# Attention with heads of width 96: the product with Wo as seven products of block sums, and a later load of the expert layer's last weights

## Chip, cores and metric

The kernel runs on one core of a Trainium2 chip. The metric is the time of one execution on the device in microseconds; runs are summed up by their median. The profile is one execution recorded by the hardware profiler, so its time is its own and is compared with itself.

## What is computed

The program is a chain of eight residual layers over 1024 tokens (16 sequences of 64) of width 512, each on a layer-normalised input. Two of them matter here, the expert layer (`L2_ffn`) and the attention after it (`L3_xattn`); the last layer (`L3_ffn`, weights of 3 bits) follows.

```python
# L2_ffn: 64 experts of rank 16, the best 16 of a token gated by a softmax
h = jnp.einsum('nd,krd->nkr', xf, A)
out = jnp.einsum('nkr,kdr->nd', h * G[:, :, None], B)      # times SCALING = 2

# L3_xattn: 16 query heads, 4 key/value heads of width 96
hidden = jnp.concatenate([context, latents], axis=1)       # 64 + 64 rows
q = (latents @ Wq.T).reshape(b, q_len, 16, 96)
k, v = (hidden @ Wk.T), (hidden @ Wv.T)                    # 4 heads each
attn = softmax(q k / sqrt(96));  out = attn v              # (b, q_len, 1536)
return out @ Wo.T                                          # 1536 -> 512
```

With four query heads to a key/value head, one key/value head gives 4 x 96 = 384 rows of Wo, three chunks of 128.

## The kernel before

**Tiles and lanes.** The tokens are eight tiles of 128 (two sequences each). The residual stream `k.x[t]` stays in SBUF. Two generators are traced into one program: lane b (`side`) does the first layers for all tiles and then the later ones for tiles 0 to 3; lane a (`main`) does the wide attention (`normed_attention`, L752) for all tiles and then the later layers for tiles 4 to 7. `merged` (L1737) interleaves them: each `yield` gives a cost in us, and the other lane is advanced until it has used as much. TensorE executes in exactly this order; the other engines and the queues are ordered by a scheduler, so a DMA goes out when its room is free and its queue (SP's) reaches it, which can be well ahead of its place in the code. Lane b is some 150 us ahead, so at the end lane a runs alone.

**Rooms.** Each lane has four PSUM banks in a ring and, for weights, four pages of 2048 floats a partition (`Lane.page`, L120); a page is free once every instruction that was given its last contents is done. Other tiles come from pools opened by each layer; `bufs` says how many there are of a tag.

**Seven products.** The expert layer's two products are already formed in Strassen's manner: over a pair of tiles and the two halves of the width, eight block products become seven. `block_sums` (L1234) forms, on GpSimd, four sums of the blocks of each weight part, and writes them to DRAM; this runs once, in lane b, one operation for each step of its `small_head_attention` (58 steps; eight parts take 33). `LoraWeights.load` (L1297) fetches a part as two DMAs, 384 KB of blocks and 512 KB of sums. `stream_sums` (L1358) and `hidden_sums` (L1420) form the sums of the activations, `Seven.products` (L1272) the products in the order a11, a12, s2, s3, s1, a22, s4, two to a bank, and `output` (L1438) adds them to the two tiles on VectorE, with one copy by ScalarE.

**The expert layer** (`lora_experts`, L1307) has parts 0 to 3 for its first product and 4 to 7 for its second. It loads 0 to 5 at its start (4 and 5 into tiles of their own) and 6 and 7 after `hidden(1, 0)`, which ends the use of parts 0 and 1. The first half of `output(0)` comes right after `hidden(1, 1)`, then `turn(1, 0)` and `turn(1, 1)` (transpositions of the gated hidden values), then the rest.

**The attention** (`packed_attention`, L1556) computes values for all tiles (with `l3a_wv`), then runs over units (head, pair of tiles), eight in a lane, head by head: `units = [(h, t) for h in range(NKV) for t in tiles[::2]]`. In iteration n it does `keys` of unit n, `turn_weights` of n-2, `scores` of n-1, `queries` of n, `project_both` of n-3 and `values` of n-2. Heads 0 to 2 carry a third of head 3's keys with them, so head 3 has no product of keys. `head_weights` loads a head's query and key weights and its rows of Wo (`l3a_o`, 768 KB) into two pages. `values` writes `aP`, three chunks for four sequences; `project` (through `Attention.project`, L742) multiplies one tile's three chunks with 128x512 of Wo into one bank, and VectorE adds the bank to `k.x[t]`. After the loop come the last unit's two `project`s, between them the pieces of the last layer (`Q3Linear`, L1498): `weights(c)` on VectorE, `norm`, `turn`, and `product` with the DMA out.

Of the kernel before, what the change touches and what calls it, by code (L numbers as in the profile page):

```python
# [8 lines left out]
F32 = mybir.dt.float32  # L9
# [9 lines left out]
P = 128  # L19
# [1270 lines left out]

class LoraWeights:

# [4 lines left out]
    def load(self, n, room=None):  # L1297
        if n in self.parts:
            return
        w = self.ln.page("w_l2f", 7 * W2) if room is None else room  # L1300
        half = 3 * W2
        self.ln.nc.sync.dma_start(w[:, :half], self.src[n, :, :half])
        self.ln.nc.sync.dma_start(w[:, half:], self.kept[n])
        self.parts[n] = w


def lora_experts(ln, tiles, weights, w_r):  # L1307
# [6 lines left out]
    with ExitStack() as es:  # L1314
        pool = ln.pool(es, "l2f")
        for n in range(4):
            weights.load(n)
        for n in range(4, 6):
            weights.load(n, pool.tile([P, 7 * W2], F32, tag=f"w{n}", name="w_l2f", bufs=1))
        wr = w_r.rearrange("p (c n) -> p c n", c=NC)  # L1320
# [37 lines left out]
        def stream_sums(p):  # L1358
            t, u = pairs[p]
            blocks = [k.kvT[:, c : c + 2, v, 1:3, :] for v in (t, u) for c in (0, 2)]  # L1360
            a11, a12, a21, a22 = blocks
            s = pool.tile([P, 4, 2, 2, S], F32, tag="s", name="sx", bufs=1)
            nc.gpsimd.tensor_tensor(s[:, 0], a21, a22, ALU.add)
            nc.gpsimd.tensor_tensor(s[:, 1], s[:, 0], a11, ALU.subtract)
            nc.gpsimd.tensor_tensor(s[:, 2], a11, a21, ALU.subtract)
            nc.gpsimd.tensor_tensor(s[:, 3], a12, s[:, 1], ALU.subtract)
            lhs[p] = {
                f"s{i + 1}": (lambda e, i=i: s[:, i, e].rearrange("p b s -> p (b s)"))
                for i in range(4)
            }  # L1370
            lhs[p]["a11"] = lambda e: k.stream(e, t)
            lhs[p]["a12"] = lambda e: k.stream(2 + e, t)
            lhs[p]["a22"] = lambda e: k.stream(2 + e, u)
# [64 lines left out]
        def output(p):  # L1438
            x = [k.x[v].rearrange("p (j n) -> p j n", j=2) for v in pairs[p]]

            def add(v, j, src):
                nc.vector.scalar_tensor_tensor(
                    x[v][:, j], src, SCALING, x[v][:, j], ALU.mult, ALU.add
                )

            m = Seven(ln, lhs.pop(p), [weights.parts[4 + e] for e in range(4)], "ps_o")
            s = pool.tile([P, 2, W2], F32, tag="u", name="uo")
            p1, p2 = m.products(2)
            nc.scalar.copy(s[:, 0], p1)
            add(0, 0, p1)  # L1450
            add(0, 0, p2)
            yield 3.45
            p6, p7 = m.products(2)
            nc.vector.tensor_tensor(s[:, 1], s[:, 0], p6, ALU.add)
            nc.vector.tensor_tensor(s[:, 0], s[:, 1], p7, ALU.add)
            yield 3.45
            p5, p4 = m.products(2)
            nc.vector.tensor_tensor(s[:, 1], s[:, 1], p5, ALU.add)
            add(1, 1, p5)
            add(1, 0, p4)  # L1460
            add(0, 1, s[:, 1])
            add(1, 1, s[:, 0])
            add(1, 0, s[:, 0])
            yield 3.45
            (p3,) = m.products(1)
            add(0, 1, p3)
            yield 1.7

# [12 lines left out]
        yield from turn(0, 0)  # L1481
        yield from hidden(1, 0)
        for n in range(6, 8):
            weights.load(n)
        yield from turn(0, 1)
        hidden_sums(0)
        yield from hidden(1, 1)
        out = output(0)
        yield next(out)
        yield next(out)  # L1490
        yield from turn(1, 0)
        yield from turn(1, 1)
        hidden_sums(1)
        yield from out
        yield from output(1)


class Q3Linear:  # L1498
# [5 lines left out]

    def load(self):
        nc, ln = self.ln.nc, self.ln
# [9 lines left out]
        self.r = r.rearrange("p (c j n) -> p c j n", c=NC, j=2)  # L1516
        self.bias = self.pool.tile([P, D], F16, tag="b16", name="b16", bufs=1)
        nc.sync.dma_start(self.bias, bias.partition_broadcast(P))
        self.wT = ln.page("wT_l3f", NC * D).rearrange("p (c n) -> p c n", c=NC)
        self.kept = {}  # L1520

    def weights(self, c):
        nc = self.ln.nc
        w, low, high = self.wT[:, c, :], self.r[:, c, 0, :], self.r[:, c, 1, :]
        nc.vector.tensor_tensor(w, high, low, ALU.subtract)
        nc.vector.scalar_tensor_tensor(
            w, self.q3[:, c * D : (c + 1) * D], 1.0 / 7.0, w, ALU.mult, ALU.mult
        )
        nc.vector.tensor_tensor(w, w, low, ALU.add)
# [14 lines left out]
    def product(self, t):  # L1544
# [3 lines left out]
        for c in range(NC):  # L1548
            nc.tensor.matmul(
                ps, lhsT=xT[:, c, :], rhs=self.wT[:, c, :], start=c == 0, stop=c == NC - 1  # L1550
            )
# [3 lines left out]

def packed_attention(ln, tiles, w_in, w_v, last):  # L1556

# [5 lines left out]
    with ExitStack() as es:  # L1563
# [31 lines left out]
        def head_weights(h):  # L1595
            if h < NKV and h not in heads:
                n_q, n_k = NC * G * HD, NC * P
                n = n_q + (n_k if h < NJ else 0)
                wa, wb = ln.page(f"l3a_w{h}", n), ln.page(f"l3a_o{h}", NJ * D)
                nc.sync.dma_start(wa, w_in[h, :, :n])  # L1600
                nc.sync.dma_start(wb, w_in[h, :, n_q + n_k :])
                heads[h] = (
                    wa[:, :n_q].rearrange("p (c n) -> p c n", c=NC),
                    wa[:, n_q:].rearrange("p (c n) -> p c n", c=NC) if h < NJ else None,
                    wb.rearrange("p (g n) -> p g n", g=NJ),
                )

        def keys(u):
            h, t = u
            if t == tiles[0]:  # L1610
                head_weights(h)
                head_weights(h + 1)
            four = k_last[:, 2 * (t - tiles[0]) : 2 * (t - tiles[0]) + 4, :]
# [49 lines left out]
        def values(u):  # L1663
            h, t = u
            d = kept[u]
            aP = pool.tile([P, NJ, 4, S], F32, tag="aP", name="aP")
            for i, pT in enumerate(d.pop("pT")):
# [9 lines left out]

        def project(u, i):
            h, t = u
            aP = kept[u]["aP"]  # L1680
            chunks = [
                aP[:, j, 2 * i : 2 * i + 2, :].rearrange("p b s -> p (b s)") for j in range(NJ)
            ]
            at.project(t + i, chunks, heads[h][2])

        def project_both(u):
            for i in range(2):
                project(u, i)

        linear = Q3Linear(ln, pool, *last)  # L1690
        units = [(h, t) for h in range(NKV) for t in tiles[::2]]
        for n in range(len(units) + 2):
            for lag, step, cost in [
# [3 lines left out]
                (0, queries, 5.2),  # L1697
                (3, project_both, 5.2),
                (2, values, 1.7),
            ]:  # L1700
                if n == len(units) + 1 and step == project_both:

# [3 lines left out]
                if 0 <= n - lag < len(units):  # L1706
                    own = step(units[n - lag])
                    yield cost if own is None else own
            if n == len(units):
                linear.load()  # L1710

# [4 lines left out]
        for c in range(2, 4):  # L1716
            linear.weights(c)
            yield 1.0
        project(units[-1], 0)
        yield 2.6  # L1720
        linear.norm(three)
        linear.turn(one)
        yield 0.5
        project(units[-1], 1)
        yield 2.6
        linear.norm(four)
        linear.turn(two)
        yield 0.5
        for t, ahead in zip(tiles, (three, four, None, None)):
            linear.product(t)  # L1730
# [48 lines left out]
def decoder_kernel(ctx: ExitStack, tc: tile.TileContext, i: dict, out: bass.AP):  # L1779
# [6 lines left out]
    kept_w = kept.tile([P, NC, D], BF16, tag="wT", name="wT_d")  # L1786
    kept_s = [kept.tile([P, 4 * W2], F32, tag=f"s{n}", name=f"sums_d{n}") for n in range(8)]

# [45 lines left out]
    def last_layers(ln, tiles, weights):  # L1834
        yield from lora_experts(ln, tiles, weights, routers[0])
        yield from packed_attention(
            ln, tiles, i["l3a_w"], i["l3a_v"], [i["l3f_q"], i["l3f_r"], i["l3f_b"], out]
        )

    def side():  # L1840
# [7 lines left out]
        with ExitStack() as es:  # L1848
            sums = block_sums(b, b.pool(es, "sums"), i["l2f_w"], kept_s)
            weights = LoraWeights(b, i["l2f_w"], kept_s)  # L1850
            for cost in small_head_attention(b, halves[0], i["l2a_w"], weights):
# [6 lines left out]
    def main():  # L1858
# [6 lines left out]
        yield from mxfp4_ffn(a, halves[1], None, i["l1f_b"], kept_w)  # L1865
        weights = LoraWeights(a, i["l2f_w"], kept_s)
        yield from small_head_attention(a, halves[1], i["l2a_w"], weights)
# [9 lines left out]
def laid_out(a):  # L1877
# [62 lines left out]
    parts = [blocks(w_a[:, D * j : D * (j + 1)], e) for j in range(2) for e in range(2)]  # L1940
    i["l2f_w"] = np.stack(parts + [blocks(w_b, e) for e in range(4)])
    w = [a[f"L3_xattn_W{n}"].T for n in "qkvo"]
    i["l3a_w"] = per_head(w[0], w[1], None, w[3], 96, 4)
    i["l3a_v"] = chunks(w[2])
# [24 lines left out]
```

## Time and profile before

| | |
|---|---|
| runs | 1619.85, 1620.28, 1628.03 us; median 1620.28 us |
| profiled execution | 1624.97 us, its span (first to last instruction) 1622.9 us |
| busy share of the span | TensorE 96%, VectorE 61%, ScalarE 38%, GpSimd 36% |
| granted TensorE clock, mean | 0.989 |
| lane b: block sums on GpSimd | 867 to 917 us |
| lane b: expert layer's products | 1050 to 1139 us |
| lane b: attention of width 96, then last layer | 1142 to 1472 us |
| lane a: expert layer's products | 1306 to 1410 us |
| lane a: attention of width 96, then last layer | 1415 to 1623 us |

In the profile's lines L12 is line 12 of the kernel; `ps_wo<-l3a_o,aP` is an instruction that writes the tile ps_wo and reads l3a_o and aP; sizes are partitions x elements; "busy, mean ns | idle before <-releaser" gives the sum of the durations, one's mean, and the time the engine stood idle before it, with the instruction that ended the idle time. PE is TensorE's matmuls, PEld its weight loads, DVE is VectorE, ACT ScalarE, POOL GpSimd, SPq the sync engine's queue, which issues all DMAs here. Matmuls are pipelined: their recorded lengths overlap, and what one costs is read from start to start. A 32-bit matmul of the code stands as two records.

### The profile page before, as it was taken

How to read it: one execution, taken by the hardware profiler on the slowest of the kernel's cores; microseconds unless marked ns; L12 is line 12 of the kernel's file. 1: busy time of each engine (PE TensorE's matmuls, PEld its weight loads, DVE VectorE, ACT ScalarE, POOL GpSimd, SP SyncE). 2: the span in 40 equal slices, each digit the busy share in tenths (PEclk: the TensorE clock that was granted, in tenths of full speed). 3: DMA queues.
4: the chain of work that ended last, by engine and by line, in shares of the span. 5: the costliest groups of instructions: out<-in, count | busy, mean ns of one | idle time of the engine just before them, and what ended most of it. 6: DMA issues, size and time to landing. Idle time of an engine off the chain costs nothing.

```text
span 1622.9 us, 21530 instructions
## 1 busy us (share of the span) xinstructions
PE 1564.4 (96%) x7291; PEld 950.1 (59%) x7296; DVE 994.2 (61%) x2084; ACT 621.5 (38%) x1944; POOL 578.4 (36%) x614
## 2 busy tenths in 40 slices
PE   7899899999999999999999999999999999999999
PEld 1234456465555645666665565667566578757774
DVE  6687587666687566777954465449345454622335
ACT  3333444244433444444443354321234433223442
POOL 2394237532286313853324433224122132111112
PEclk9999999999999999999999999999999999999999
DMA  8892349623695345944435622214220113201120
GB/s 233 269 288 88 115 145 266 193 83 102 191 271 159 108 142 168 272 156 176 170 129 206 230 76 92 79 46 179 72 69 21 36 73 128 64 26 46 39 72 26
DMA packets 104237, 215.06 MB, mean 133 GB/s; under 512 B 49600, under 2 KB 66752, under 8 KB 93504
## 3 DMA queue, kind: packets, MB, share of 16 engines
q1 hardware_dynamic: 104128, 213.68, 41.8%
q8 instruction: 59, 0.97, 0.2%
q14 instruction: 50, 0.41, 0.1%
HBM read 190.06 MB, written 23.59 MB: 132 GB/s over the span
## 4 chain that ended last, share of the span: by engine, by line
PE 77%; DVE 12%; DMA 4%; ACT 3%; POOL 2%; issue 2%; SPq 0%; ACTq 0%; POOLq 0%; DVEq 0%
PE ps_wo L746 15%; PE ps_q L860 10%; PE ps_kv L878 5%; PE ps_q L1636 5%; PE ps_ckv L812 5%; PE ps_a L737 4%; PE ps_s L696 4%; PE ps_pT L143 3%; PE ps_o L1279 3%; DMA att<-att_d 3%; PE ps_h L1279 3%; PE ps_v L1583 3%; PE ps_k L1620 3%; PE ps_wo L1206 2%; PE ps_q L1138 2%
## 5 line engine op out<-in xcount | busy, mean ns | idle before, releaser
L746 PE MATMUL ps_wo<-l1a_o,aT 128*128 128x512 f32 x512 | 233.6, 599 | 3.1 <-ACT aT L930 3.1
L860 PE MATMUL ps_q<-l1a_w,kvT 128*128 128x512 f32 x512 | 233.0, 598 | 0.0
L712 ACT ACTIVATE p<-ps_s,mx 128x128 f32<-128x128 f32 x384 | 135.4, 369 | 221.1 <-DVE mx L707 204.9
L721 POOL TENSOR_TENSOR p<-p,sm 128x512 f32<-128x512 f32 x96 | 103.7, 1081 | 301.2 <-DVE sm L720 270.5
L125 POOL TENSOR_TENSOR r<-r,mhalf 128x5 f32<-128x5 f32 (+1 forms) x96 | 101.9, 1062 | 222.6 <-DVE r L802 219.4
L860 PEld LDWEIGHTS ps_q<-l1a_w,kvT 128*128 128x128 f32 x512 | 96.3, 192 | 116.7 <-issue 115.2
L746 PEld LDWEIGHTS ps_wo<-l1a_o,aT 128*128 128x128 f32 x512 | 93.6, 192 | 101.5 <-issue 96.8
L159 DVE TENSOR_TENSOR x<-x,ps_wo 128x512 f32<-128x512 f32 x104 | 70.6, 679 | 112.5 <-PE ps_wo L746 78.4
L878 PE MATMUL ps_kv<-l1a_w,kvT 128*128 128x256 f32 x512 | 122.7, 383 | 2.7 <-DVE x L159 2.7
L478 POOL TENSOR_TENSOR acc<-acc,pv 128x512 f32<-128x512 f32 x96 | 121.5, 1291 | 4.4 <-DVE pv L468 3.7
L812 PE MATMUL ps_ckv<-l1a_kv,kvT 128*64 128x512 f32 x512 | 116.9, 598 | 4.4 <-ACT ckv L821 4.4
L801 DVE TENSOR_REDUCE r<-sq 128x5 f32<-128x640 f32 x64 | 52.3, 817 | 103.7 <-ACT sq L886 103.7
L878 PEld LDWEIGHTS ps_kv<-l1a_w,kvT 128*128 128x128 f32 x512 | 92.7, 191 | 19.1 <-DVE x L159 4.3
L868 ACT ACTIVATE sq<-ps_q 128x512 f32<-128x512 f32 x64 | 38.2, 598 | 151.4 <-PE ps_q L860 151.4
L468 DVE TENSOR_TENSOR pv<-att,ps_v 128x512 f32<-128x512 f32 x128 | 82.1, 677 | 22.4 <-DMA att<-att_d 17.8
L125 POOL TENSOR_TENSOR rs<-rs,mhalf 128x1 f32<-128x1 f32 x64 | 37.7, 595 | 162.4 <-DVE rs L134 157.9
L696 PE MATMUL ps_s<-kT,qT 128*128 128x128 f32 (+1 forms) x704 | 91.5, 275 | 0.0
L371 DVE TENSOR_TENSOR prod<-qs,kp 128x1024 f32<-128x1024 f32 x64 | 80.9, 1301 | 14.5 <-ACT qs L352 7.6
L696 PEld LDWEIGHTS ps_s<-kT,qT 128*128 128x128 f32 (+1 forms) x704 | 85.1, 192 | 2.3 <-issue 0.9
L1636 PE MATMUL ps_q<-kvT,l3a_w 128*128 128x256 f32 x384 | 85.5, 379 | 0.0
L746 PE MATMUL ps_wo<-l3a_o,aP 128*128 128x512 f32 x192 | 85.5, 593 | 0.0
L728 DVE COPY pT<-ps_pT 128x512 f32<-128x512 f32 x96 | 64.3, 682 | 31.3 <-PE ps_pT L143 31.1
(216 smaller groups left out, 2856.2 us busy)
## 6 DMA issues: line engine op xcount, KB each, us to landing
l1a_w<-in_l1a_w SPq DMA_DIRECT2D x32, 1536.0 KB, 7.3
att<-att_d SPq DMA_DIRECT2D x64, 512.0 KB, 9.3
l1a_o<-in_l1a_w SPq DMA_DIRECT2D x32, 1024.0 KB, 5.2
s<-ckv SPq DMA_DIRECT2D x32, 256.0 KB, 4.5
w_l2f<-sums_d SPq DMA_DIRECT2D x16, 512.0 KB, 5.5
w_l2f<-in_l2f_w SPq DMA_DIRECT2D x16, 384.0 KB, 4.3
l3a_w<-in_l3a_w SPq DMA_DIRECT2D x6, 1024.0 KB, 6.5
l3a_o<-in_l3a_w SPq DMA_DIRECT2D x8, 768.0 KB, 4.3
```

What stands on the lines that cost most here:

```text
L125: self.nc.gpsimd.tensor_tensor(out, v, self.k.mhalf[:, : v.shape[1]], ALU.pow)
L468: nc.vector.tensor_tensor(pv.rearrange("p (q w n) -> p q w n", w=2, n=L), att[:, a, :].rearrange("p (q w n) -> p q w n", w=2, n=L), spaced ...
L478: nc.gpsimd.tensor_tensor(sums, before, pv, ALU.add)
L696: nc.tensor.matmul(ps[:, i, :], lhsT=qT[:, i // 2, 2 * (i % 2) : 2 * (i % 2) + 2, :].rearrange("p g s -> p (g s)"), rhs=kTs[i // 2], start ...
L712: nc.scalar.activation(p[:, i, :], ps[:, i, :], AF.Exp, bias=mx[:, i : i + 1], scale=self.scale, accum_out=sm[:, i : i + 1],)
L721: nc.gpsimd.tensor_tensor(p, p, bc(sm, 2, P), ALU.mult)
L746: self.nc.tensor.matmul(ps, lhsT=a, rhs=wo[:, g, :], start=g == 0, stop=g == len(chunks) - 1)
L812: nc.tensor.matmul(ps[j * S : (j + 1) * S], lhsT=k.context(c, 2 * t + 1 - j), rhs=w_pair[hp][:, c, :], start=c == 0, stop=c == NC - 1,)
L860: nc.tensor.matmul(ps, lhsT=k.stream(c, t), rhs=w_qkv[n][0][:, c, :], start=c == 0, stop=c == NC - 1,)
L878: nc.tensor.matmul(ps, lhsT=k.stream(c, t), rhs=w_qkv[n][1][:, c, :], start=c == 0, stop=c == NC - 1,)
L1279: self.ln.nc.tensor.matmul(ps[:, i % 2], lhsT=a(e), rhs=w[:, b * W2 : (b + 1) * W2], start=e == 0, stop=e == len(self.rhs) - 1,)
L1636: nc.tensor.matmul(ps[:, j], lhsT=wq[:, c, (j0 + j) * P : (j0 + j + 1) * P], rhs=k.kvT[:, c, t : t + 2, 1:3, :], start=c == 0, stop=c == N ...
```

## The change

Both products with Wo and the expert layer's second product now share one function, `add_seven`, and one class of weights, `BlockWeights` (the old `LoraWeights`, with 14 parts where there were 8; parts 8 to 10 are Wo's rows for heads 0 and 1, 11 to 13 for heads 2 and 3). A pair of heads takes the place that the two halves of the width had: the blocks are (tile t, head h-1), (t, h), (t+1, h-1), (t+1, h), each three chunks deep.

```diff
+def add_seven(ln, m, s, x, factor, cost):
...
+    p1, p2 = m.products(2)
+    nc.scalar.copy(s[:, 0], p1)
+    add(0, 0, p1)
+    add(0, 0, p2)
+    yield cost
+    p6, p7 = m.products(2)
+    nc.vector.tensor_tensor(s[:, 1], s[:, 0], p6, ALU.add)
+    nc.vector.tensor_tensor(s[:, 0], s[:, 1], p7, ALU.add)
+    yield cost
+    p5, p4 = m.products(2)
+    nc.vector.tensor_tensor(s[:, 1], s[:, 1], p5, ALU.add)
+    add(1, 1, p5)
+    add(1, 0, p4)
+    add(0, 1, s[:, 1])
+    add(1, 1, s[:, 0])
+    add(1, 0, s[:, 0])
+    yield cost
+    (p3,) = m.products(1)
+    add(0, 1, p3)
+    yield cost / 2
```

In the expert layer, parts 4 to 7 all go into pages and are loaded later, the second product stands behind both transpositions, and one sum of `stream_sums` is made in place in `k.kvT` (the four GpSimd operations stay four):

```diff
         for n in range(4):
             weights.load(n)
-        for n in range(4, 6):
-            weights.load(n, pool.tile([P, 7 * W2], F32, tag=f"w{n}", name="w_l2f", bufs=1))
...
         yield from hidden(1, 0)
+        yield from turn(0, 1)
+        for n in range(4, 6):
+            weights.load(n)
+        hidden_sums(0)
+        yield from hidden(1, 1)
         for n in range(6, 8):
             weights.load(n)
-        yield from turn(0, 1)
-        hidden_sums(0)
-        yield from hidden(1, 1)
-        out = output(0)
-        yield next(out)
-        yield next(out)
+        yield 3.0
         yield from turn(1, 0)
+        yield 3.0
         yield from turn(1, 1)
         hidden_sums(1)
-        yield from out
+        yield 2.0
+        yield from output(0)
         yield from output(1)
```

In the attention, the units run in pairs of heads, `head_weights` loads no Wo, `out_weights` loads a pair's three parts after iterations 1 and 7 (two into pages, one into a tile of a new pool `late`, opened after iteration 1, which also holds `aP`), `sums` forms the sums of `aP` on GpSimd, and `project_half` runs the first four products of a pair in one iteration and the other three in the next:

```diff
-        units = [(h, t) for h in range(NKV) for t in tiles[::2]]
+        units = [(2 * p + j, t) for p in range(NKV // 2) for t in tiles[::2] for j in range(2)]
+        ahead = {units[0]: (0, 1), units[3]: (2,), units[4]: (3,)}
...
+                s = late.tile([P, 3, NJ, 2, S], F32, tag="sa", name="sa", bufs=1)
+                nc.gpsimd.tensor_tensor(s[:, 1], a11, a21, ALU.subtract)
+                nc.gpsimd.tensor_tensor(a21, a21, a22, ALU.add)
+                nc.gpsimd.tensor_tensor(s[:, 0], a21, a11, ALU.subtract)
+                nc.gpsimd.tensor_tensor(s[:, 2], a12, s[:, 0], ALU.subtract)
...
+        def project_half(u):
+            if u[0] % 2:
+                running.append(project(u))
+                return next(running[0]) + next(running[0])
+            if running:
+                return sum(running.pop())
+            return 0.0
...
-                (3, project_both, 5.2),
+                (3, project_half, 5.2),
                 (2, values, 1.7),
+                (2, sums, 0.0),
...
+            if n in (1, 7):
+                late = late or ln.pool(es, "l3b")
+                out_weights(n // 7)
             if n == len(units):
-                linear.load()
+                linear.load(pool)
...
-        project(units[-1], 0)
-        yield 2.6
-        linear.norm(three)
+        yield project_half(units[-1])
         linear.turn(one)
         yield 0.5
-        project(units[-1], 1)
-        yield 2.6
+        yield project_half(units[0])
+        linear.norm(three)
         linear.norm(four)
         linear.turn(two)
         yield 0.5
-        for t, ahead in zip(tiles, (three, four, None, None)):
+        for t, ahead in zip(tiles, (None, three, four, None)):
```

The last layer's weights, which had a page, and its bias go into tiles that the attention's `qT` and `kT` leave. `block_sums` runs over 14 parts. The two tiles of a pair get their last contribution of a pair of heads together, so `norm(three)` comes after all products of the last pair.

## The prediction

> **What bounds the kernel now.** I read the page first, then TensorE's instructions in order of time over the stages that the change touches, then the table by stretches, the table of DMA issues and the waits of the sync queue. The page says that TensorE is the bound, and gives the row that is replaced (the second L746 row) and a row of the shape that replaces it (L1636):
>
> ```profile
> PE 1564.4 (96%) x7291; PEld 950.1 (59%) x7296; DVE 994.2 (61%) x2084; ACT 621.5 (38%) x1944; POOL 578.4 (36%) x614
> ...
> L1636 PE MATMUL ps_q<-kvT,l3a_w 128*128 128x256 f32 x384 | 85.5, 379 | 0.0
> L746 PE MATMUL ps_wo<-l3a_o,aP 128*128 128x512 f32 x192 | 85.5, 593 | 0.0
> ```
>
> Each product in the code is two records, so 96 products with Wo give 192. Neither row waits. In order of time, lane a's end, where no other lane is left, looks like this (start, length, what):
>
> ```profile
> 1573.41 5.31 PE L746 MATMUL ps_wo<-l3a_o,aP 128*128 128x512 f32 x12
> 1578.56 1.89 PE L737 MATMUL ps_a<-pT,v_all 128*96 128x256 f32 x8
> ...
> 1583.24 5.32 PE L746 MATMUL ps_wo<-l3a_o,aP 128*128 128x512 f32 x12
> 1588.39 1.89 PE L737 MATMUL ps_a<-pT,v_all 128*96 128x256 f32 x8
> ```
>
> TensorE is dense even with one lane: from 1475 to 1580 us it is busy 104.94 of 105 us. A microsecond taken out of it there is a microsecond off the end, as long as nothing else becomes late. The other touched stage, lane b's expert layer, is the one place with real gaps:
>
> ```profile
> 1107.75 3.62 PE L1279 MATMUL ps_o<-w_l2f,sh 128*128 128x256 f32 x16
> 1111.20 0.39 PE L143 MATMUL ps_mx<-ident,q 128*128 128x128 bf16 x4
> 1111.42 1.04 PE L143 MATMUL ps_hT<-ident,hg 128*128 128x128 f32 x8
> 1113.96 1.07 PE L143 MATMUL ps_hT<-ident,hg 128*128 128x128 f32 x8 [1.50 <-DVE x L1442]
> 1116.74 6.46 PE L1279 MATMUL ps_o<-w_l2f,hT 128*128 128x256 f32 x16 [1.71 <-DVE uo L1455]
> ```
>
> ```profile
> 1112.00:1116.00 4.00, 1.53 (x13) 1.09 (x11) 4.00 (x9) 2.26 (x5) 0.93 (x1) 0.94 1.00 416
> 1116.00:1120.00 4.00, 3.26 (x8) 2.63 (x9) 4.00 (x13) 0.00 (x0) 0.42 (x1) 0.50 0.29 117
> 1120.00:1125.00 5.00, 5.00 (x20) 4.21 (x19) 3.08 (x9) 0.00 (x0) 2.21 (x2) 0.77 0.00 0
> ```
>
> (Busy PE, PEld, DVE, ACT, POOL, then granted clock, DMA share, GB/s.) VectorE is full with lane a's MXFP4 layer, TensorE waits 3.2 us for it, and then 16 records take 6.46 us where the 16 above take 3.62: the granted clock is 0.50, which loses another 2.8 us.
>
> **Term 1, the products with Wo.** Starts, not record lengths, tell what one costs: 1583.24 to 1588.39 is 5.15 us for 12 records of 128x512, 0.429 each; 1107.75 to 1111.20 is 3.45 us for 16 records of 128x256, 0.216 each. For two heads and two tiles, before: 2 x 12 records x 0.429 = 10.30 us. After: 7 products x 3 chunks x 2 records = 42 x 0.216 = 9.07 us. That is 1.23 us saved, eight times (four in each lane): -9.8 us. The other bound is from busy means: ps_o<-w_l2f,hT has 31.9 us for 128 records, 0.249 each, so 336 records cost 83.7 us against 85.5, -1.8 us; but that mean counts the slow stretch above and the overlap of neighbouring groups, so I take -9.8.
>
> **What the new form adds on other engines.** VectorE: 4 adds of 128x512 (679 ns, L159) become 11 operations of 128x256 (416 ns, L1442 and L1454), 2.7 to 4.6 us for a pair; ScalarE gets one copy of 0.37 us. GpSimd gets four operations of 128x384, between 0.73 us (128x256, L1363) and 1.3 us (128x512, L1424): about 1.0 each, 4 us for a pair. In the steady loop an iteration of some 15 to 18 us of TensorE covers this: VectorE is busy 36.9 of the 105 us named above, GpSimd 14.6, and the sums made at the end of an iteration are needed only at the third product of the next. I cost it at 0 there. Without that cover, each pair would show GpSimd's chain of two operations behind the last copy, about 2 us.
>
> **Term 2, lane a's end.** There the cover is thin. The last `values` is followed at once by products 1 and 2 (12 records, 2.6 us); product 3 needs two GpSimd operations one after the other, which start when ScalarE's aP copies end, 1.9 us after `values`. That is 1.9 + 2 x 1.0 to 1.4 = 3.9 to 4.7 us against 2.6: a wait of 1.3 to 2.1 us. VectorE also gets some 5 us more adds in the stretch where it makes the last layer's weights:
>
> ```profile
> 1589.00:1603.00 14.00, 13.98 (x49) 7.57 (x48) 13.49 (x26) 5.54 (x17) 3.79 (x4) 1.00 0.00 1
> ```
>
> Four banks and 7.7 us of products between tile three's last add and its transposition absorb most of it. I take +3 us, bounds 0.5 and 6. What is late next is `norm(three)`, with that slack.
>
> **Term 3, lane b's expert layer.** Loads 4 and 5 move from the layer's start to behind `turn(0,1)` and take the pages of parts 0 and 1, free at 1096.9; loads 6 and 7 move past `hidden(1,1)` and take the pages of parts 2 and 3, free at about 1103.9. Each load is two DMAs (0.33 and 0.43 us of the sync queue). `output(0)` needs part 7's first third before its first product ends. The yields of 3, 3 and 2 us hand the time to the other lane, which at this place only has the MXFP4 layer, almost nothing for TensorE. How long the load takes:
>
> ```profile
> l3a_wv<-in_l3a_v SPq DMA_DIRECT2D x1, 768.0 KB, 6.0
> w_l2f<-sums_d SPq DMA_DIRECT2D x1, 512.0 KB, 13.1
> ```
>
> Those two were issued at 1103.9 and 1106.5. Load 6 and 7 take the place of the first in the queue, with 1.3 MB until the first need, at 0.4 MB/us (the 416 GB/s above) plus the rest of what is under way: 6 to 7 us, so 1110 to 1111. By the place of the second it would be 1117. The gates of `hidden(1,1)` end on GpSimd at 1110 anyway, and `turn(1,1)` waits for them. So: TensorE ends `hidden(1,1)` at 1104.2, has about 1.3 us of transpositions, idles some 5 us, does both `output`s from 1111.4 in 24.2 us, 2.5 us of slow clock, 2.6 us of lane a's products and 1 us of waits for banks: 1141.7 against 1139.0 now. +2.7 us; bounds -3 (only today's waits go) and +8 (load at 1117). Queued behind the waiting loads on the sync queue are lane a's w_l2q and w_l2o, first used at 1167 and 1246: nothing. `hidden_sums(1)` has one buffer, so it still waits for `output(0)`'s last product; its chain of 1.3 + 0.7 + 0.7 us lies under products 1 and 2 (3.45 us): 0. In lane a the same yields get lane b's attention: 0.
>
> The Trainium skill ("TensorE: Matmul & The Clock Gate", Part 1) has the clock halved after an idle window of about 3.4 us. The row shows 0.50 after two waits of 1.50 and 1.71 us with a little work between, so here less than an unbroken 3.4 us was enough. By the rule the old order should have kept its clock and the new idle of 5 us should lose it, which would make this term about 2.8 us worse than mine; the row says that both lose it.
>
> **Term 4, l3a_wv.** Its page now comes from part 4, free only when `output(1)` ends; 768 KB land in 4.8 to 6.0 us, and the first product with it came 3.4 us (lane b) and 4.3 us (lane a) after that end: 0 to 2 us a lane, I take 0.4 each, +0.8.
>
> **Term 5, six more block sums.** 24 GpSimd operations and 12 DMAs of 512 KB, spread over all steps of lane b's small-head attention:
>
> ```profile
> L1252 POOL TENSOR_TENSOR sums<-sums 128x256 f32<-128x256 f32 x32 | 22.9, 738 | 20.3 <-DMA sums<-in_l2f_w 19.7
> SPq L1254 <- POOL sums L1252: 22.1, 6, 6.4
> ```
>
> The eight parts ran from 867 to 917, 6.1 us each, so fourteen end at about 953, before lane b's expert layer at 1050. From 867 to 917 GpSimd stood waiting for DMA with other work behind it, and TensorE lost only 0.7 us. +1 us, bounds 0 and 15.
>
> **At nothing.** The second pair's weights: loads are issued as soon as a page is free (the q3 load, asked for after iteration 8, went out at 1563.74, when a page came free in iteration 6). Parts 11 and 12 get the pages of the query weights before the last product of iteration 7; only part 13 waits for it, needs about 3.5 us (768 KB took 4.3), and is wanted 5.6 us later. If all three began there, TensorE would wait about 2.3 us. The in-place sums, the order of heads, the tile places: 0.
>
> **Sum.** -9.8 + 3 + 2.7 + 0.8 + 1 = -2.3 us. The profiled execution took 1624.97 us (span 1622.9), so 1622.7 by its own clock; the median shown is 4.7 us lower, and 1620.28 - 2.3 is 1618.
>
> **Rivals.** (a) The saving arrives whole: terms 2 to 5 vanish in slack, and the two waits at 1112 to 1117 go: -9.8 - 3 + 0.5 = -12.3, 1608 us. For it: the dense rows. Against: VectorE's 96% near the end, the sparse lane at 1104. (b) Slower: the six more sums, between 917 and 953. GpSimd is in order, and there it also has lane b's softmax (L1175) and lane a's r (L125), whose result reaches TensorE's next transposition with some 4 to 5 us to spare; waits for DMA were 3.3 us in the mean, 5.1 at the longest. From a hold-up past that slack, each part costs 2.5 us: 6 x 2.5 = 15 in place of 1, 1632 us. Against: the first eight did no such harm. (c) The seven products save nothing, because a 128x256 record really costs 0.249: -1.8 in place of -9.8, 1626 us, still within the bound below.
>
> **Chances.** A measurement of this kernel can tell about 0.5% (8.1 us) from no change. My forecast, 1618, with its own range 1612 to 1624, and (c), both within it: 0.48. (a) and what lies towards it, faster by more: 0.27. (b) and a late load 6/7 on top of it, slower by more: 0.25. The range 1607 to 1632 reaches to both other cases.
>
> **What would show it.** ps_wo of this layer with 336 records of 128x256 at 0.216 us from start to start; the wait before product 3 near the end; an idle of 4 to 6 us after `hidden(1,1)` near 1105 with the clock at 0.5 behind it; the sums row with 56 operations that end near 953 and no TensorE waits before. Wrong would be a sums row that makes ps_qT or ps_pT wait, a load of parts 6 and 7 that lands after 1117, or a wait before the products of the second pair of heads.

## The result and the profile after

| | before | after |
|---|---|---|
| median of the runs made side by side | 1620.17 us | 1635.28 us |
| ratio of the runs, 95% interval | | 1.0086, 1.0060 to 1.0112 |
| profiled execution, its span | 1624.97, 1622.9 us | 1636.32, 1634.5 us |
| granted TensorE clock, mean | 0.989 | 0.985 |

The changed kernel is 0.6 to 1.1% slower, and 1635.3 us lies outside the predicted range of 1607 to 1632. The page of the changed kernel first, its busy times and the row of the shape that did not change:

```profile
PE 1563.4 (96%) x7435; PEld 982.3 (60%) x7440; DVE 1017.8 (62%) x2140; ACT 625.5 (38%) x1952; POOL 631.6 (39%) x670
...
L1651 PE MATMUL ps_q<-kvT,l3a_w 128*128 128x256 f32 x384 | 85.6, 379 | 0.0
```

The products with Wo now stand in two rows of the groups (busy, mean ns | idle before):

```profile
L1279 PE MATMUL ps_wo<-w_sums,aP 128*128 128x256 f32 x192 | 44.1, 379 | 0.0
...
L1279 PE MATMUL ps_wo<-w_sums,sa 128*128 128x256 f32 x144 | 36.4, 401 | 3.0 <-POOL sa L1701 3.0
```

336 records of 128x256, as predicted, and TensorE's busy time is the same as before (1564.4), which says little: a record that runs at half clock is busy for twice as long. So the two traces are compared in another way. For each matmul the time from its start to the next one's start is taken; the median of that over all records of its shape in both traces is its price (0.429 us for 128x512, 0.216 for 128x256, 0.109 for 128x128). What is left over is idle time or slow clock, and is called the loss here. Summed from one fixed product to another (times of the kernel before):

```
stage                                              loss before   after
start to 925 (no line of it is changed)                210.54    208.64
the next 35.9 us of priced records                       3.66     15.41
to the end of hidden(1,1) in lane b, 1104               10.02     10.02
lane b's expert layer, to its l3a_wv products, 1142      8.40      8.51
to lane a's expert layer, 1302                          20.18     19.09
lane a's expert layer, 1415                              0.98      3.31
end of lane b, lane a's values, 1472                     0.10      2.80
lane a's attention, to its last values, 1596             1.24      1.23
lane a's end                                             0.47      8.44
price of all records                                  1356.22   1346.42
```

The price fell by 9.8 us. Against that stand +11.75, +0.11, -1.09, +2.33, +2.70, -0.01 and +7.97 in the stages behind 925, 23.8 us in all: +14.0 us, and the ratio of the runs is worth 13.9. The first stage is left out of that sum, since it varies by itself: in thirteen traces of this study, whose TensorE work up to there is the same, it lost 202.7 to 212.5 us.

The first loss, in the order of time on GpSimd (start, length, what, and the idle time before):

```profile
922.30 5.75 POOL L1252 TENSOR_TENSOR sums<-sums 128x256 f32<-128x256 f32 x8 [4.73 <-DMA sums<-in_sums_w]
928.01 1.17 POOL L125 TENSOR_TENSOR r<-r,mhalf 128x5 f32<-128x5 f32 x1
...
938.01 5.51 POOL L1252 TENSOR_TENSOR sums<-sums 128x256 f32<-128x256 f32 x8 [2.86 <-DMA sums<-in_sums_w]
943.49 2.04 POOL L1175 TENSOR_TENSOR p<-p,sm 128x512 f32<-128x512 f32 x2
945.50 1.16 POOL L125 TENSOR_TENSOR r<-r,mhalf 128x5 f32<-128x5 f32 x1
```

VectorE and then TensorE in the same stretch:

```profile
929.21 0.69 DVE L901 TENSOR_TENSOR qn<-qn,r 128x512 f32<-128x512 f32 x1 [6.16 <-POOL r L125]
...
946.69 0.69 DVE L901 TENSOR_TENSOR qn<-qn,r 128x512 f32<-128x512 f32 x1 [6.53 <-POOL r L125]
```

```profile
930.05 0.73 PE L143 MATMUL ps_qT<-ident,qn 128*128 128x128 f32 x4 [2.43 <-DVE qn L901]
931.94 3.78 PE L878 MATMUL ps_kv<-l1a_w,kvT 128*128 128x256 f32 x8 [0.94 <-DVE x L159]
950.18 0.63 PE L143 MATMUL ps_pT<-ident,p 128*128 128x128 f32 x4 [3.13 <-DVE p L1170]
```

GpSimd takes its instructions in a fixed order. VectorE has finished the input of lane a's `r` at 918.60, but `r` starts at 928.01: ahead of it stand the rest of the wait of 4.73 us for a transfer and eight sums, 5.75 us. So VectorE stands 6.2 us for `r` with everything else behind, and TensorE waits in turn. Then eight records of 128x256 take 3.78 us where 1.89 is usual: the granted clock is 0.50 there. The second `r` is 6.7 us late (input at 938.77, start at 945.50), and no wait for a transfer lies in that time, only sums and two operations of lane b's softmax. Of the 11.75 us some 6.5 are waits of TensorE (the three above); the rest, 5.3, is put down to the slow clock.

The second loss, at lane a's end:

```profile
1599.97 0.99 POOL L1700 TENSOR_TENSOR aP<-aP 128x384 f32<-128x384 f32 x1 [2.35 <-ACT aP L1690]
...
1600.92 1.60 POOL L125 TENSOR_TENSOR rs<-rs,mhalf 128x1 f32<-128x1 f32 x2
1602.04 2.08 DVE L1536 SCALAR_TENSOR_TENSOR wT_l3f<-w_l3f,wT_l3f 128x512 f32<-128x512 int32 x2
1602.50 1.07 POOL L1701 TENSOR_TENSOR sa<-aP 128x384 f32<-128x384 f32 x1
1603.62 5.49 PE L1279 MATMUL ps_wo<-w_sums,sa 128*128 128x256 f32 x12 [3.03 <-POOL sa L1701]
...
1622.25 3.70 PE L1559 MATMUL ps_o<-wT_l3f,xT 128*128 128x512 f32 x8 [0.73 <-ACT xT L1551]
...
1627.12 3.70 PE L1559 MATMUL ps_o<-wT_l3f,xT 128*128 128x512 f32 x8 [0.73 <-ACT xT L1551]
```

The two sums that product 3 needs have `norm`'s two `rs` between them, product 3 waits 3.03 us, and its 12 records take 5.49 us instead of 2.75. The stretches around it (busy PE, PEld, DVE, ACT, POOL, then granted clock, DMA share, GB/s) show the halved clock and a VectorE that is full:

```profile
1600.00:1604.00 4.00, 0.97 (x4) 0.57 (x3) 4.00 (x4) 0.37 (x1) 3.92 (x5) 0.86 0.00 0
1604.00:1609.00 5.00, 5.00 (x13) 3.82 (x13) 5.00 (x9) 0.00 (x0) 3.31 (x2) 0.50 0.00 0
```

Later each of the last two products waits 0.73 us, because the transposition of its tile now stands directly ahead of it. Lane b's end shows the same, as 0.73 and 1.45 us.

Lane b's expert layer, where the prediction expected a long idle time (TensorE):

```profile
1116.44 0.66 PE L143 MATMUL ps_hT<-ident,hg 128*128 128x128 f32 x4 [1.99 <-DVE uh L1422]
...
1119.56 1.54 PE L143 MATMUL ps_hT<-ident,hg 128*128 128x128 f32 x6 [2.02 <-POOL hg L1417]
1120.89 5.65 PE L1279 MATMUL ps_o<-w_sums,hT 128*128 128x256 f32 x16
1126.38 3.62 PE L1279 MATMUL ps_o<-w_sums,sh 128*128 128x256 f32 x16
```

The waits are for VectorE's and GpSimd's work on the gated values, and no record waits for the parts loaded later.

### The profile page after: what moved, and what is told of

Same layout as the page of the kernel before. It is cut to its first block, busy times and chain, and to the rows that moved or that the text cites. A ratio compares the mean times of both kernels' runs of the same rounds, so it can differ in the third digit from the quotient of the medians.

```text
span 1634.5 us, 21987 instructions
## 1 busy us (share of the span) xinstructions
PE 1563.4 (96%) x7435; PEld 982.3 (60%) x7440; DVE 1017.8 (62%) x2140; ACT 625.5 (38%) x1952; POOL 631.6 (39%) x670
## 4 chain that ended last, share of the span: by engine, by line
PE 72%; DVE 12%; DMA 5%; POOL 4%; ACT 4%; issue 3%; SPq 1%; ACTq 0%; DVEq 0%; POOLq 0%
PE ps_q L860 9%; PE ps_wo L746 9%; PE ps_kv L878 5%; PE ps_q L1651 5%; PE ps_ckv L812 5%; PE ps_wo L1279 4%; PE ps_s L696 4%; PE ps_a L737 4%; PE ps_o L1279 3%; PE ps_pT L143 3%; PE ps_v L1593 3%; PE ps_h L1279 2%; PE ps_k L1635 2%; DMA att<-att_d 2%; PE ps_o L1559 2%
## 5 line engine op out<-in xcount | busy, mean ns | idle before, releaser
L159 DVE TENSOR_TENSOR x<-x,ps_wo 128x512 f32<-128x512 f32 x72 | 48.7, 676 | 57.1 <-PE ps_wo L1206 33.8
L712 ACT ACTIVATION_READ_ACCUMULATOR p<-ps_s,mx 128x1 f32 x384 | 79.6, 207 | 0.0
```

The source lines that it names most:

```text
L712: nc.scalar.activation(p[:, i, :], ps[:, i, :], AF.Exp, bias=mx[:, i : i + 1], scale=self.scale, accum_out=sm[:, i : i + 1],)
```

## Experiments on the sums

**Left out** (e1_eight_sums).

```diff
-    n_parts = src.shape[0]
+    n_parts = 8
...
-        self.ln.nc.sync.dma_start(w[:, half:], self.kept[n])
+        self.ln.nc.sync.dma_start(w[:, half:], self.kept[n] if n < 8 else self.src[n])
```

> Starts from the changed kernel (1635.3 us). The block sums of the six parts of Wo are left out: block_sums runs over eight parts only, and a part of Wo takes its second 512 KB from the unsummed blocks, so the products with Wo read the wrong right-hand sides; the number of products, loads on the later side and all orders stay. Theory S (the six parts' sums hold GpSimd's queue, and lane a's r behind them, between 924 and 961): the 11.8 us lost there come back, 1623 to 1624.5 us, VectorE's two waits of 6 us for r are gone. Rival L (the loss comes from the expert layer's later loads and the end of lane a): 1634 to 1636. Rival M (the sums cost half of it, the rest is the DMA traffic or a slower clock that stays): about 1629.

This kernel forms no sums of Wo's six parts, so it does not compute the layer; only its time is of use. Measured: median 1621.62 us, ratio to the kernel before 1.0004 (0.9985 to 1.0024). The stage at 925 loses 3.65 us, as in the kernel before; every later stage up to lane a's end is as in the changed kernel to about 0.1 us, and that end loses 6.9. Theory S holds.

**Moved** (e2_sums_later): eight parts in the small-head attention, six more in lane b's packed attention.

```diff
+        if ln.name == "b":
+            more = block_sums(ln, ln.pool(early, "sums2"), w_out.src, w_out.kept, 8, 14)
...
                 nc.scalar.copy(v_all[:, 2 * i + j, :], ps)
+                for _ in range(4):
+                    next(more, None)
                 yield 2.6
```

> The same six parts are summed, but later: in lane b's attention of width 96, four steps after each of the eight products of values (about 1160 to 1200 us), in rooms of their own that are given back before the products with Wo begin. Theory S: as in e1, 1623 to 1626 us, because GpSimd has next to nothing else there. If the sums cost what they cost wherever they stand (24 operations of 0.74 us beside VectorE, 12 transfers of 512 KB): 1633 to 1636. If they become late for the first load of Wo's parts, TensorE waits before the first product with Wo: above 1636.

Measured: 1620.27 us, ratio 0.9995 (0.9975 to 1.0015); the stage at 925 loses 3.66 us, and the stage at 1142 to 1302 is the same to 0.01 us as without the sums (e1). GpSimd there:

```profile
1158.85 5.73 POOL L1251 TENSOR_TENSOR sums<-sums 128x256 f32<-128x256 f32 x8 [8.69 <-DMA sums<-in_sums_w]
1170.87 5.75 POOL L1251 TENSOR_TENSOR sums<-sums 128x256 f32<-128x256 f32 x8 [6.28 <-DMA sums<-in_sums_w]
1185.77 2.04 POOL L1175 TENSOR_TENSOR p<-p,sm 128x512 f32<-128x512 f32 x2 [9.16 <-DVE sm L1174]
```

It waits longer than at 922, and nobody loses by it: GpSimd's next operation waits 9.16 us for VectorE, so nothing stood ready behind the sums. The price is not that of the work but of what stands behind it in the queue.

**Two loads under way** (e3_sums_ahead).

```diff
-    load(0)
+    load(0)
+    load(1)
...
-            for out, v, w in ((0, b12, b11), (1, b22, t[0]), (2, b22, b12), (3, b21, t[1])):
+            steps = ((b11, b12, b11), (b12, b22, b12), (b22, b22, b11), (b21, b21, b22))
```

> The fourteen parts are summed where they are now, but in place (a room of 4 KB a partition in place of 8, four rooms in place of two) and with two loads under way instead of one, so GpSimd should no longer stand waiting for a transfer with r behind it. Same number of GpSimd operations, same bytes. Theory S1 (it is the waiting for the transfers in GpSimd's queue): a part takes 3 to 3.5 us instead of 6, 8 to 12 us come back, 1623 to 1627. Theory S2 (it is GpSimd's work itself, 16 sums in a row ahead of r, or VectorE slowed beside it): 3 us or less come back, 1632 to 1636.

Measured: 1623.25 us, ratio 1.0011 (0.9991 to 1.0031); the stage at 925 loses 3.65 us. The group of sums, over the whole span:

```profile
L1255 POOL TENSOR_TENSOR sums<-sums 128x256 f32<-128x256 f32 x56 | 41.2, 743 | 9.3 <-DMA sums<-in_sums_w 6.1
```

For the changed kernel that row reads:

```profile
L1252 POOL TENSOR_TENSOR sums<-sums 128x256 f32<-128x256 f32 x56 | 40.1, 742 | 30.2 <-DMA sums<-in_sums_w 29.3
```

Same operations, same 0.74 us each, but the waiting for transfers fell from 29.3 to 6.1 us, and all 56 are done at 925, before the small scores' softmax begins to share GpSimd. S1's time came true and S2's did not. But this does not show that the waiting alone is the cause: the shorter wait brings the earlier end, so the sums' own work has left the stretch too, and of the 9.4 us by which `r` was late 5.75 were sums. The same trace shows what a late `r` costs earlier (GpSimd and VectorE):

```profile
885.12 5.43 POOL L1255 TENSOR_TENSOR sums<-sums 128x256 f32<-128x256 f32 x7 [1.99 <-DMA sums<-in_sums_w]
890.50 1.18 POOL L125 TENSOR_TENSOR r<-r,mhalf 128x5 f32<-128x5 f32 x1
891.71 1.20 DVE L901 TENSOR_TENSOR qn<-qn,r 128x512 f32<-128x512 f32 x1 [4.13 <-POOL r L125]
```

This `r`, whose input VectorE finished at 883.16, is 7.3 us late, and VectorE stands 4.1 us for it; yet TensorE's loss over the 60 us ahead of the small-head scores is 1.6 us, as in the kernel before and in the changed one. An `r` 6.7 us late at 945 made TensorE wait 3.13 us.

**Alone** (e9_six_more_sums_alone), in the kernel before.

```diff
-    n_parts = src.shape[0]
+    n_parts = 14
...
-            nc.sync.dma_start(rooms[n][:, 0], src[n])
+            nc.sync.dma_start(rooms[n][:, 0], src[n % 8])
```

> The kernel before with one part of the change alone: block_sums runs over fourteen parts (the last six read parts 0 to 5 again, and nobody uses what they write). Everything else as before. Theory S1: the six more parts cost by themselves what the changed kernel lost there: the stretch between the first scores of lane b's small-head attention and 40 us of work later loses 14 to 16 us instead of 3.7, the time is about 1632 to 1634 us. Rival C (the loss needs the new products' other traffic or order too): under 1627.

Measured, one run: 1634.01 us; the stage at 925 loses 15.1 us, all stages after 1142 are those of the kernel before to 0.1 us. The six parts cost 11.5 us by themselves, and need nothing else of the change.

## Experiment on the later loads

**The expert layer's part alone** (e6_lora_alone), in the kernel before; the edit is the second diff of the change, without the sum made in place.

> The kernel before (1620.2 us) with one part of the change alone: the expert layer's weights 4 to 7 loaded later into pages and its second product behind both transpositions, with the yields of the change; products with Wo and eight block sums as before. By the prediction's term 3: +2.7, about 1623. By the stages of the changed kernel's trace (idle and slow clock in lane b's expert layer +0.2, in lane a's +2): 1620 to 1623. By the rival of a late load: 1625 to 1628.

Measured: 1618.32 us, ratio 0.9973 (0.9955 to 0.9992): not a loss but 1.3 to 7.3 us won. By stages: lane b's expert layer loses 7.4 instead of 8.4 us, 1142 to 1302 loses 16.2 instead of 20.2, lane a's expert layer 2.7 instead of 1.0. The first difference says little: in the eleven traces with this order that stage lost some 6.7 to 8.5 us. In the second, two waits of TensorE that the kernel before has are gone:

```profile
1212.27 0.63 PE L143 MATMUL ps_pT<-ident,p 128*128 128x128 f32 x4 [1.97 <-DVE p L1170]
...
1258.09 0.63 PE L143 MATMUL ps_pT<-ident,p 128*128 128x128 f32 x4 [1.97 <-DVE p L1170]
```

The order in which TensorE takes the two lanes' work between 1142 and 1302 differs between the two traces, some 100 us behind the edit; no part of the edit is aimed there. That the new yields shift it, and that the new order is what removes the waits, fits this but was not tried by itself. In lane a's expert layer the loss of e6 stands at its start, within some 10 us; its products with parts 4 to 7 lose nothing.

## Experiments on lane a's end

**Order of the seven products** (e4_product_order): `a11, a12, s3, a22, s2, s1, s4`, so that the first four need only `s3`, the first sum made. p7's bank is kept until p6 is there.

```diff
+        p7, p4 = m.products(2)
+        add(1, 0, p4)
+        yield cost
+        p6, p5 = m.products(2)
+        nc.vector.tensor_tensor(s[:, 1], s[:, 0], p6, ALU.add)
+        nc.vector.tensor_tensor(s[:, 0], s[:, 1], p7, ALU.add)
```

> The changed kernel with the products with Wo in another order, a11, a12, s3, a22, s2, s1, s4, so that the first four need nothing of the last operation but one on GpSimd (s3 is ready 2.4 us before the last values' copies end); the adds on VectorE stay eleven. Theory O (only the order is wrong at lane a's end): the wait of 3.03 us and the slow clock behind it go, the idle and slow clock from lane a's last values on fall from 8.4 to about 3 us. Rival X (the normalised x of the first tile is as late as the sum): TensorE now stands before the transposition of xn, until about 1606 us on the changed kernel's time axis, some 3 us, and 6 to 8 of the 8.4 us stay. In the steady loop 0 in both.

Measured, one run: 1637.06 us. Lane a's end loses 9.7 us; both theories miss, rival X by less. TensorE's waits in lane a:

```profile
1534.17 2.05 PE L696 MATMUL ps_s<-kT,qT 96*128 96x128 f32 x16 [0.62 <-ACT aP L1699]
...
1607.95 1.11 PE L143 MATMUL ps_xT<-ident,xn 128*128 128x128 f32 x4 [5.37 <-DVE xn L136]
```

The wait for the sum is gone and a longer one for `xn` stands a few records later. And a bank held longer costs 0.62 us three times in lane a's attention, which was expected at 0: its stage loses 4.2 instead of 1.2.

**Order of the transpositions** (e5_turns_together).

```diff
         yield project_half(units[-1])
-        linear.turn(one)
-        yield 0.5
         yield project_half(units[0])
...
+        linear.turn(one)
+        yield 0.5
...
-        for t, ahead in zip(tiles, (None, three, four, None)):
+        for t, ahead in zip(tiles, (None, (three, four), None, None)):
```

> The changed kernel with the order after the last unit changed: both halves of the last pair's products, then the transpositions of tiles one and two, products one and two, transpositions three and four, products three and four. The waits of 0.73 and 1.45 us (lane b) and 0.73 and 0.73 us (lane a) before products three and four shrink to one of about 0.3 us a lane: the stage 1424 to 1476 loses 1 instead of 2.8 us, lane a's end 7 instead of 8.4; the wait of 3.03 us before product 3 of the last pair and its slow clock stay. Rival: the waits only move before transposition one, both numbers stay as they are.

Measured, one run: 1631.19 us. Lane b's end loses 1.15 us, as expected (1 expected, 2.8 before the edit); lane a's end loses 8.0 where 7 was expected: the waits before the last products shrink to 0.24 and 0.29 us, but product 3 now waits 3.60 us and the first transposition 0.97 us. With the end unedited this stage lost between 6.6 us (e2) and 8.4 us (the changed kernel), so a change of 0.4 us in its total says nothing by itself.

**Both** (e45_both); the edits are those two.

> Both edits of the end together on the changed kernel. Theory: four products and then the other three cover both the last sum and xn, so lane a's end loses 2 to 3 us instead of 8.4 and lane b's 1 instead of 2.8; the whole is 7 to 8 us under the changed kernel in span outside the stage before 924 us. Rival: VectorE's adds come so late that the end is bound by them, and lane a's end loses 5 us or more.

Measured, one run: 1640.83 us; lane a's end loses 11.6 us, so the rival's case: VectorE's adds for the last pair start more than 10 us after its first products, behind the last layer's weights, and TensorE waits for them.

```profile
1599.17 2.75 PE L1280 MATMUL ps_wo<-w_sums,aP 128*128 128x256 f32 x12
...
1613.42 0.41 DVE L1300 TENSOR_TENSOR x<-x,ps_wo 128x256 f32<-128x256 f32 x1
1614.82 1.12 PE L143 MATMUL ps_xT<-ident,xn 128*128 128x128 f32 x4 [6.38 <-DVE x L1300]
```

**The last layer's weights early** (e7_early_weights), in lane a alone.

```diff
+            if ln.name == "a" and n == 2:
+                linear.load(ln.pool(es, "l3f"))
+            if ln.name == "a" and 4 <= n < 8:
+                linear.weights(n - 4)
```

> The changed kernel, with the last layer's weights in lane a in rooms of their own (24 KB a partition of what lane b has given back by then): the loads go out after iteration 2 and VectorE makes one chunk of the weights after each of the iterations 4 to 7, in place of all twelve operations among the last adds and normalisations. Lane b, and the order of TensorE, as in the changed kernel. Theory V (at lane a's end VectorE is late because those twelve operations, 0.65 to 1.07 us each, stand among its adds): the idle and slow clock from lane a's last values on fall from 8.4 to 4 or 5 us, and what is left is the wait for the last pair's sum on GpSimd, about 3 us with a slow clock behind it, or less of it, as GpSimd's ops get shorter without VectorE beside them. Rival G (only GpSimd's chain decides): 7 to 9 us as before. Both leave the stages before alone.

Measured, one run: 1634.06 us; lane a's end loses 6.3 us, between the two theories, but little below the 6.6 us that e2 lost with an unedited end. What is clear is the wait: GpSimd's `rs` between the two sums takes 1.17 instead of 1.60 us, and product 3 waits 2.42 us instead of 3.03, with a slow clock behind it.

```profile
1602.84 4.33 PE L1279 MATMUL ps_wo<-w_sums,sa 128*128 128x256 f32 x12 [2.42 <-POOL sa L1706]
```

With the order changed (e45) VectorE was late, with the weights alone GpSimd is.

**With the order and the transpositions** (e8_early_and_order). p7 is now added at once, by a twelfth add, so its bank is free:

```diff
+        p7, p4 = m.products(2)
+        nc.vector.tensor_tensor(s[:, 1], s[:, 0], p7, ALU.add)
+        add(1, 0, p4)
+        yield cost
+        p6, p5 = m.products(2)
+        nc.vector.tensor_tensor(s[:, 1], s[:, 1], p6, ALU.add)
+        nc.vector.tensor_tensor(s[:, 0], s[:, 0], p6, ALU.add)
```

> The last, with the tail's order (all products of the last pair, then transpositions one and two) and the products with Wo in the order a11, a12, s3, a22, s2, s1, s4, now with a twelfth add that gives s3's bank back at once. Theory V: with VectorE free, the first four products cover GpSimd's chain, and lane a's end loses 2 us or less; the two waits of 0.62 us in the steady loop of the other run with this order are gone. Rival X (xn is late whatever VectorE does, by GpSimd's rs behind the sums): lane a's end loses 5 us or more, at the first transposition.

Measured, one run: 1626.44 us. Lane a's end loses 1.2 us instead of 8.4, the loop 1.2, lane b's end 1.1. VectorE's first add of the last pair now starts 6.4 us after its first products, where it was 14.3 us in e45; this add stands ahead of the twelfth. What the twelfth add does for the end by itself was not tried. What is left of waits there:

```profile
1605.42 7.13 PE L1577 MATMUL ps_o<-wT_l3f,xT 128*128 128x512 f32 x16 [0.24 <-ACT xT L1569]
1613.72 7.13 PE L1577 MATMUL ps_o<-wT_l3f,xT 128*128 128x512 f32 x16 [0.29 <-ACT xT L1569]
```

**All together** (e10_combined): e2 and e8 on the changed kernel.

> The changed kernel with the four edits together: the six parts of Wo summed in lane b's attention of width 96; the last layer's weights early in lane a; products with Wo in the order a11, a12, s3, a22, s2, s1, s4; all products of the last pair ahead of the transpositions, these in twos. By the stages of the single runs: 1635.3 - 11.8 (sums) - 7.2 (lane a's end) - 1.7 (lane b's end) = 1614.6 us, 0.4 to 0.5% faster than the kernel before. If the edits disturb each other: 1618 to 1622, no difference.

Measured: 1614.21 us against 1622.58 of the kernel before, run beside it, ratio 0.9951 (0.9933 to 0.9969): the edits add up, and this version is 0.3 to 0.7% faster than the kernel before.

## Why the prediction was wrong

**Term 1 was right**: 336 records at 0.216 us from start to start. That the price of all records fell by 9.79 us against 9.8 predicted is the same sum once more, with the same two prices; what tests it is that nothing was lost again around them. In lane a's attention the loss is 1.23 us against 1.24, so the cover in the loop held too: the extra work of VectorE and GpSimd costs 0.0 us there.

**Term 5 is the step that failed.** "+1 us, bounds 0 and 15" rested on the first eight parts having done no harm; the runs show 11.5 to 11.8 us. The prediction had most of the mechanism, as its rival (b): a hold-up in GpSimd's queue with lane a's `r` behind it. It priced that at 15 us and gave it, together with a late load, 0.25. It put the hold-up down to the waits for DMA; the rows show the sums' own work as the larger part of it. What should have decided is that the stretch differs: until 917 GpSimd serves lane a and the sums alone, while from 920 lane b's softmax needs it too. That the six parts cause the loss, in that queue at that place, is shown from both sides (e1, e2, e3 take it away, e9 makes it). That the place decides is shown by e2, and by e3's `r` that is 7.3 us late near 890 and costs TensorE nothing; that it is TensorE's want of other work that makes a late `r` hurt after 920 was argued and not tried by itself.

**Term 2 had the right mechanism and too small a size.** The wait before product 3 was put at 1.3 to 2.1 us and is 3.03, since `rs` stood between the two sums. The slow clock behind it, which the prediction knew from lane b's expert layer, was not counted here; it took 2.7 us in the changed kernel's trace, 1.6 us in e1's and 0.1 us in e2's, after the same wait. The end lost 6.1 to 8.0 us over the runs, against +3 with bounds 0.5 and 6. "Absorb most of it" was wrong for VectorE: its twelve operations for the weights were pushed from 1589 to 1600, among the adds; moving them, the product order, the twelfth add and the transpositions together took 7 us away.

**Not seen**: the new order of the loop's last lines puts each transposition directly ahead of its product. The prediction has no term for it; it costs lane b's end 2.18 us of waiting, of which the edit of e5 gives 1.65 back.

**Term 3 had the wrong sign.** +2.7 was predicted; alone the later loads win 3.2 us by stages. The load was never the limit, as the prediction had it, but the 5 us of idle time were two waits of 2 us. The win at 1142 to 1302 and the loss in lane a's expert layer lie where no term looked; the interleaving is the likely cause and is not shown to be. In the changed kernel lane b's stages up to 1302 make -1.0 us together and lane a's expert layer +2.3, of which 1.4 stand at the router's first products and 0.9 before `l3a_wv`, with nothing lost between.

**Term 4**: the wait before the first `ps_v` grew from 0.34 to 0.57 us and from 0.65 to 1.27, +0.85 against +0.8; but what releases it is the normalised stream (`kvT`), not the load, and with the later loads alone (e6) the two waits are 0.29 and 0.66 us. So the number agreed by luck.

The sum of terms 2 to 5 was +7.5; the stages behind 925 show +23.8.

## What to carry to other kernels

Work added to an engine that takes its instructions in order costs what it makes late, so look at what stands behind each wait of that queue where the work will land, not at what the same work did elsewhere; issue loads for such work two ahead, or put it where the queue is empty. A microsecond of waiting costs nearly two when the clock halves behind it, which it does in some executions and not in others. Where a kernel's tail shortens, count the operations of every engine in the tail: they had been hidden by what was taken away or by their place.

## What the runs showed of the hardware

**A wait of 2 to 3 us can halve the clock, and need not.** For e7, stretches with busy PE, PEld, DVE, ACT, POOL, then granted clock:

```profile
1600.40:1602.80 2.40, 0.02 (x1) 0.00 (x0) 1.38 (x2) 0.37 (x1) 2.39 (x4) 0.93 0.00 0
1602.80:1605.00 2.20, 2.16 (x5) 1.80 (x6) 1.02 (x3) 0.00 (x0) 2.13 (x2) 0.50 0.00 0
```

One wait of 2.42 us is followed by a clock of 0.50. In e2 the longer wait of 3.03 us before the same product is not: its 12 records take 2.86 us, and the clock stays at 1.00.

```profile
1587.86 2.86 PE L1278 MATMUL ps_wo<-w_sums,sa 128*128 128x256 f32 x12 [3.03 <-POOL sa L1708]
1587.80:1590.00 2.20, 2.14 (x10) 1.91 (x11) 2.20 (x3) 0.00 (x0) 1.33 (x2) 1.00 0.00 0
```

A wait of 2.2 us near 637, the same in both main traces, is followed by 0.50 in the kernel before and by 1.00 in the changed one. The Trainium skill ("TensorE: Matmul & The Clock Gate", Part 1) puts the idle window at about 3.4 us; here less was enough in some traces.

**VectorE and GpSimd slow each other.** At lane a's end the pair of L1536 operations took 2.08 us while GpSimd worked on its sums at 1602, and 1.28 us at 1608; there it was GpSimd whose additions of the bias took 6.12 us for two, against 2.26 us in e7, where the weights are gone from that place.

```profile
1608.16 1.28 DVE L1536 SCALAR_TENSOR_TENSOR wT_l3f<-w_l3f,wT_l3f 128x512 f32<-128x512 int32 x2
1606.66 6.12 POOL L1545 TENSOR_TENSOR x<-x,b 128x512 f32<-128x512 f32 x2 [1.69 <-DVE xn L136]
...
1603.89 2.26 POOL L1550 TENSOR_TENSOR x<-x,b 128x512 f32<-128x512 f32 x2
```

(The first two are the changed kernel's, the third is e7's.) The Trainium skill ("GPSIMD Engine Reference", 1. Specifications) has the two engines share their SBUF interfaces, with contention for VectorE instructions that read two SBUF inputs; these VectorE operations read two SBUF tiles, and the rows agree.
